# Turning half of the first pair's context among the last expert blocks, in memory lent from the blocks' side

## The chip, the core and the metric

The kernel runs on one core of a Trainium2 chip. The metric is the time of one execution in device microseconds, and times are compared as medians of several runs. One execution was also recorded by the hardware profiler; every position in microseconds below is counted from the start of that execution's span.

The engines are TensorE (PE; its weight loads are PEld), VectorE (DVE), ScalarE (ACT), GpSimd (POOL) and SyncE (SP), which issues most of the direct DMAs. Each engine works through its own list in order.

## What is computed

The program is a two-layer block on 32 sequences of 56 tokens (width 256), with a context of 1500 rows of 256 for each sequence. Cut to its four steps:

```python
x = x + L0_xattn(layernorm(x), ctx)          # a decayed scan over the context, averaged, as one row per sequence
x = x + L0_ffn(layernorm(x), ...)            # 16 experts, the 6 best of each token, hidden width 176
x = x + L1_xattn(layernorm(x), ctx, mask)    # softmax attention of 56 queries over 1500 context rows
x = x + L1_ffn(layernorm(x), ...)            # 2 experts, the best of each token, hidden width 1024
```

The third step is the one at which the change sits:

```python
scores = einsum('bsd,bmd->bsm', hidden_states, memory_tokens) * scale
scores = where(memory_mask[:, None, :], scores, -1e30)
attn = softmax(scores); readout = einsum('bsm,bmd->bsd', attn, memory_tokens)
```

## The kernel before

The 32 sequences are worked in 16 pairs, so that two times 64 query rows fill the 128 partitions. There are four stages: a first pass over all contexts (to about 200 us), the 99 expert blocks of the first expert layer (to about 456 us), the attention over the 16 pairs (to about 697 us), and the blocks of the second expert layer.

**The first expert layer.** `expert_blocks` walks over `NB0` = 99 blocks of 128 sorted rows. A step t multiplies block t by gate and up weights on PE (L723), ACT applies the silu (`sg`), DVE multiplies (`hs`, L735), PE turns `hs` of block t-1, DVE copies it out (`hT`, L743), and PE multiplies block t-2 by the down weights (`y`, L750). ACT copies `y` to `yb`, and SP writes `yb` to the array `ys0` in main memory (`ys<-yb`, L886). All weights lie in one tile, `w0_sb`, of 77,824 bytes in each partition. At the end of each step `side(t)` is called, which puts other work among the blocks in written order: the indices that bring the rows back (`ways`, working in the tiles `ra`, `rt1`, `t8s`), a row of constants (`zrow`) that is written to main memory, the gathers of the first five pairs' results by POOL (`results`, tiles `g` of the pool `res0`, summed by `added`), the queries of pairs 0 and 1, the first five contexts into the five slots of `ring`, and at step `NB0 - 4` the preparation of the second sort (`for_second_sort`).

**The attention.** A context of one sequence is a tile of 128 partitions by 3072 values (12 chunks of 256; 1.5 MB). There are eight slots: five in `ring` and three more, `extra0` to `extra2`, of the pool `at`, which takes memory that the blocks have used. `transposed(b, n)` is one DVE instruction (L1016) that turns half n of context b into a tile `cT`; `turn(p, n)` does so for the two contexts of a pair. `scores` multiplies 128 small matmuls for a pair (L1055): the first 64 read the `cT` tiles of half 0, the last 64 those of half 1. `mask_terms(p)` loads the pair's mask by SP (`mu`), and `mask_added` lets ACT make of it the tile `mf` of additive terms (L1038, L1043). `masked` adds `mf` on DVE and takes the maximum (L1068), `softmax` is ACT's exponential (L1080), `turned` turns the probabilities on PE (L1095), and `attend` multiplies them by the context (`op`, L1103) and then loads the pair four places on into the two slots that have come free. Of that loop the part around which the prediction turns is:

```python
cTs = [turn(0, 0), turn(0, 1)]
mask_added(mu_.pop(0))
for p in range(NP + 1):
    ...                                  # roots and query rows of pair p + 2, its mask
    sps = scores(cTs, xqs.pop(p))
    lo = turn(p + 1, 0)
    sc, mx = masked(sps)
    nb = softmax(sc, mx)
    cTs = [lo, turn(p + 1, 1)]
    ...                                  # attend pair p - 1, gathers of pair p + 5, queries of pair p + 2
    held = (p, turned(sc), nb)
    mask_added(mu_.pop(p + 1))
```

**What sets the order.** All engines are under a manual schedule: each engine's list is in the order in which the code is written, and only semaphores lie between engines. SP's list is one queue for masks, contexts and `ys<-yb`. Memory is taken by pools that are opened and closed like a stack. A pool that is opened over the memory of closed ones waits, with its first use by an engine, for all that still works in the closed ones under it. Before the attention `w0_sb` and the pools of the blocks are closed, and `so`, `pay`, `at`, `ctxT` (four `cT` tiles) and `res1` are opened over them, in this order. So `at` lies in what was `w0_sb`, and `ctxT` beyond it, over the blocks' working tiles, `yb` and `zrow` among them. At the start of the attention SP issues the two first masks and then the three `extra` contexts.

Of the kernel before, what the change touches and what calls it, by code (L numbers as in the profile page):

```python
# [8 lines left out]
F32 = mybir.dt.float32  # L9
U8 = mybir.dt.uint8  # L10
# [8 lines left out]
P = 128  # L19
B, S, D, T = 32, 56, 256, 1500  # L20
KD = D // P
NP = B // 2
TOK = 2 * S
NM, JM = 3, 4
NCH = NM * JM
TS = (T - P * JM) // (NM - 1)
TD = P * JM - TS
Q = 32
NE = D // Q
CW = NCH * D  # L30
NRING, NXTRA = 5, 3
E0, F0, K0 = 16, 176, 6
# [6 lines left out]
NE0 = 5  # L39
# [3 lines left out]
NB0 = (B * S * K0 + E0 * (P - 1)) // P  # L43
NY1 = 3
NB1 = B * S // P + 1
WP = 2 * D + 2
# [8 lines left out]
def xattn_ffn_kernel(  # L55
# [22 lines left out]
    nc = tc.nc  # L78
    V, A, PE, G = nc.vector, nc.scalar, nc.tensor, nc.gpsimd
# [3 lines left out]
    at2 = ctx.enter_context(tc.tile_pool(name="at2", bufs=2))  # L83
# [16 lines left out]
        out=before, in_=before, compare_op=ALU.is_gt, fill=0.0,  # L100
# [41 lines left out]
    slots = [ring[:, i, :].rearrange("p (j d) -> p j d", d=D) for i in range(NRING)]  # L142

    def load_ctx(b, c):
        nc.sync.dma_start(
            out=c.rearrange("p (m j) d -> p m (j d)", j=JM),
            in_=bass.AP(cx.tensor, b * T * D, [[JM * D, P], [TS * D, NM], [1, JM * D]]),
        )
# [56 lines left out]
    with tc.tile_pool(name="p1", bufs=1) as p1, tc.tile_pool(name="p3", bufs=3) as p3, tc.tile_pool(  # L205
        name="xn", bufs=4
    ) as xnp, tc.tile_pool(name="z", bufs=4) as zp, tc.tile_pool(name="p1_ps", bufs=5, space=PSUM) as ps, tc.tile_pool(
        name="p1_acc", bufs=2, space=PSUM
# [63 lines left out]
        q, r = divmod(TD, JM)  # L272
# [504 lines left out]
    def levels_of(p):  # L777

        return (TOK * (p + 1) - 1) // P + 1

    def results(pool, p, n, i):

        g = pool.tile([P, K0 // 2, D], F32, tag="g", name="g")
        for k in range(K0 // 2):
            G.indirect_dma_start(  # L785
                out=g[:, k, :], out_offset=None, in_=ys0[0 : n * P, :],
                in_offset=bass.IndirectOffsetOnAxis(
                    ap=back[:, p, 3 * i + k : 3 * i + k + 1], axis=0
                ),
            )  # L790
        return g
# [50 lines left out]
    def queries(pool, ps, tag, xn, half, xq=None):  # L842
# [10 lines left out]
        A.copy(xq[:, NE // 2 * half : NE // 2 * (half + 1), :].rearrange("p e c -> p (e c)"), tp)  # L853
        return xq

    mvq, xqs = {}, {}
    gd = at2.tile([P, D], F32, bufs=1, name="gd")
    toks = at2.tile([P, NP], F32, bufs=1, name="toks")
# [3 lines left out]
    with tc.manual_schedule(  # L862
        engines={ET.PE, ET.DVE, ET.Activation, ET.SP, ET.Pool}
    ), tc.tile_pool(name="f0", bufs=3) as wk, tc.tile_pool(name="f0r", bufs=1) as rt, tc.tile_pool(
        name="f0x", bufs=5
    ) as xbp, tc.tile_pool(name="res0", bufs=2) as resp, tc.tile_pool(
        name="f0_tr", bufs=2, space=PSUM
    ) as ptr, tc.tile_pool(name="f0_gu", bufs=2, space=PSUM) as pgu, tc.tile_pool(
        name="f0_ht", bufs=2, space=PSUM
    ) as pht, tc.tile_pool(name="f0_y", bufs=2, space=PSUM) as py:  # L870
        zrow = rt.tile([P, WP], F32, name="zrow")
        G.memset(zrow, 0.0)
        G.memset(zrow[:, WP - 1 : WP], float(FAR))

# [11 lines left out]
            nc.sync.dma_start(out=ys0[i * P : (i + 1) * P, :], in_=yb)  # L886


        ra = rt.tile([P, NP, E0], F32, name="ra")
        rt1 = rt.tile([P, NP, E0], F32, name="rt1")  # L890
        t8s = rt.tile([P, NP, 8], F32, name="t8s")

        def ways(a, b):
            n = b - a
# [25 lines left out]
        gs = {}  # L920
        ways_ = [f for a, b in ((0, NE0), (NE0, NP)) for f in ways(a, b)]

        mvs, steps = {}, {}

        gcol = rt.tile([P, KD], F32, name="gcol")

# [11 lines left out]

        def side(t):

            if t == NB0 - 4:
                for_second_sort()
            if t > 1:
                for _ in range(3):
                    if ways_:
                        next_ = ways_.pop(0)
                        next_()
            if t % 3 == 0 and 0 < t <= 3 * NRING:
                load_ctx(t // 3 - 1, slots[t // 3 - 1])
            if t % 3 == 0 and 0 < t - 3 * NRING <= NB1:  # L950
                j = t - 3 * NRING
                nc.sync.dma_start(
                    out=xs1.rearrange("(p j) d -> p j d", j=NB1)[:, j - 3 : j, :],
                    in_=zrow.unsqueeze(1).to_broadcast([P, 3, WP]),
                )
            for p in range(NE0):
                t0 = E0 * levels_of(p) + 4
                if t in (t0, t0 + 2):
                    gs.setdefault(p, []).append(
                        results(resp, p, E0 * levels_of(p), (t - t0) // 2)  # L960
                    )
                if t == t0 + 8:
                    added(p, gs.pop(p))
                if p >= 3:
                    continue
                if t == t0 + 14:
                    mvq[p] = stats1(xr[:, p, :])
                if p >= 2:
                    continue
                if t == t0 + 15:  # L970
                    steps[p] = list(roots_by_steps(mvq[p]))
                for _ in range(4):
                    if steps.get(p):
                        steps[p].pop(0)()
                if t == t0 + 20:
                    mvs[p] = query_rows(p, mvq[p])
                if t == t0 + 21:
                    xqs[p] = queries(at2, ptr, "tr", mvs[p], 0)
                if t == t0 + 22:
                    queries(at2, ptr, "tr", mvs[p], 1, xqs[p])  # L980
# [10 lines left out]
    payp = ctx.enter_context(tc.tile_pool(name="pay", bufs=7))  # L991
    with tc.manual_schedule(
        engines={ET.PE, ET.DVE, ET.Activation, ET.SP, ET.Pool}
    ), tc.tile_pool(name="at", bufs=1) as at, tc.tile_pool(
        name="ctxT", bufs=4
    ) as ctp, tc.tile_pool(name="res1", bufs=2) as resp, tc.tile_pool(
        name="at_sc", bufs=1, space=PSUM
    ) as psc, tc.tile_pool(name="at_pt", bufs=3, space=PSUM) as ppt, tc.tile_pool(
        name="at_o", bufs=1, space=PSUM
    ) as po:  # L1000
        for i in range(NXTRA):
            c = at.tile([P, NCH, D], F32, name=f"extra{i}")
            slots.append(c)
        NS = NRING + NXTRA
        mf = at.tile([P, NCH, P], F32, name="mf")
        G.memset(mf[:, JM:NCH, 0 : TD // JM + 1], -BIG)
        mus = [at.tile([P, T], U8, name=f"mu{i}") for i in range(2)]
        nbig = at.tile([P, 1], F32, name="nbig")
        G.memset(nbig, -BIG)
        gap = so.tile([1, 1], F32, name="gap")  # L1010
        A.preload_act_table_set("natural_log_exp_and_others")

        def transposed(b, n):

            cT = ctp.tile([P, NCH, NE // 2, Q], F32, tag="cT", name="cT")
            V.transpose(  # L1016
                out=cT.rearrange("p j e q -> p j (e q)"),
                in_=slots[b % NS][:, :, P * n : P * n + P],
            )
            return cT  # L1020

        def mask_terms(p):

            mu = mus[p % 2]
            nc.sync.dma_start(
                out=mu, in_=bass.AP(mask.tensor, 2 * p * T, [[T, 2], [0, 64], [1, T]])
            )
            return mu

        mu_ = {p: mask_terms(p) for p in range(2)}  # L1030
        for b in range(NRING, NS):
            load_ctx(b, slots[b])

        def mask_added(mu):
            q, r = divmod(TD, JM)
# [196 lines left out]
                tc.add_to_no_dep_group("xs1", g.ins)  # L1232

        def turn(p, n):
            return [transposed(2 * p + h, n) for h in range(2)]

        def apart():

# [4 lines left out]
                results(*queue[sent[0]])  # L1243
                sent[0] += 1

        cTs = [turn(0, 0), turn(0, 1)]
        mask_added(mu_.pop(0))
        mvs, four, late = {}, [], []
        held = None
        for p in range(NP + 1):  # L1250
            if p == NP - 1:
                order_of_blocks()

            if p + 2 < NP:
                roots(mvq[p + 2])
            if p - 2 in mvs:
                roots(mvs[p - 2])
            if p + 2 < NP:
                xn = query_rows(p + 2, mvq.pop(p + 2))
                mu_[p + 2] = mask_terms(p + 2)  # L1260
            if p - 2 in mvs:
                sort_norm(p - 2, mvs.pop(p - 2))
            if p < NP:
                sps = scores(cTs, xqs.pop(p))
                if p + 1 < NP:
# [3 lines that stand above are left out]
                if p + 1 < NP:  # L1269
                    cTs = [lo, turn(p + 1, 1)]  # L1270
                inverse(mx, nb)
            if held:
                op = attend(held[0], held[1])
                mvs[held[0]] = sort_rows(held[0], op, held[2])
                held = None

            for i in range(2):
                if p + NE0 < NP:
                    fresh = results(resp, p + NE0, NB0, i)
                if late:  # L1280
                    half_added(*late.pop())
                if p + NE0 < NP:
                    late.append((p + NE0, fresh))
            if p + 3 < NP:
                mvq[p + 3] = stats1(xr[:, p + 3, :])
            if p + 2 < NP:
                xqs[p + 2] = queries(at2, ppt, "pt", xn, 0)
                queries(at2, ppt, "pt", xn, 1, xqs[p + 2])
            if four:
                sort_place(*four[0], sort_rank(four.pop()[1], ppt, "pt"))  # L1290
            if 0 <= p - 2 < NP:
                sort_gate(p - 2)
                if (p - 2) % GP == GP - 1:
                    o = p - 2 - GP + 1
                    four.append((o, sort_four(o)))
            if p < NP:
                held = (p, turned(sc), nb)
            if p + 1 < NP:
                mask_added(mu_.pop(p + 1))
            if p == NP - 1:  # L1300
                for i in range(NY1):
                    apart()
                    rows_of1(i, payp, "pay")
# [110 lines left out]
```

## Time and profile before

| | |
|---|---|
| median of six runs | 885.63 us (882.16 to 890.86) |
| profiled execution | 879.96 us, its span 878.2 us |
| mean granted TensorE clock | 0.959 |
| PE busy | 801.5 us, 91% of the span |
| DVE, ACT, POOL busy | 55%, 39%, 45% |
| last matmul of the first blocks, first scores | 455.6 us, 460.15 us |
| direct loads on SP's queue | 139.55 MB, 45.6% of 16 DMA engines' span |

How to read it: the share of busy time is a mean over stages that have different limits. The change sits at one seam, between two stages in which PE is nearly always busy, so the lines to look at are those around 456 us, engine by engine. The chain of waits names, from the end backwards, what released each step. In the timeline the square brackets hold the idle time before an instruction and what ended it. The granted clock is the share of full speed at which TensorE was let run.

### The profile page before, as it was taken

To read this page: it belongs to the slowest core of one execution; us is meant where nothing else is said; L and a number is where in the kernel's file an instruction comes from. 1 tells how busy PE (TensorE), PEld (TensorE's weight loads), DVE (VectorE), ACT (ScalarE), POOL (GpSimd) and SP (SyncE) were. 2 spreads that over 40 slices of the span, in tenths; PEclk is the share of its full clock that TensorE was granted. 3 is DMA by queue.
4 is the path that set the end of the run, shared out by engine and by line. 5 is a ranking of instruction groups with operands and counts; after the bars stand their busy time and mean duration, and the time that the engine had idled before them with its cause. 6 is when DMAs were issued, how large, how long until landed. Compare 5 with 4: busy or idle time off the path is not lost.

```text
span 878.2 us, 18685 instructions
## 1 busy us (share of the span) xinstructions
PE 801.5 (91%) x6658; PEld 527.9 (60%) x6658; DVE 481.1 (55%) x1419; ACT 343.3 (39%) x902; POOL 398.7 (45%) x497
## 2 busy tenths in 40 slices
PE   4688888878999999999978999899998999999997
PEld 4345555545777777777754666555655556665664
DVE  3487777873542424332237888778979333323332
ACT  0133333323444444444435675764766311111110
POOL 4455565425347656565717886288400230111110
PEclk9799999968999999999997999899999999999999
DMA  9999999933987534344528796797975720110010
GB/s 264 348 397 382 334 391 354 322 124 105 318 293 248 153 108 138 103 142 116 124 73 297 244 329 229 244 324 262 318 249 179 255 85 13 36 37 27 29 37 12
DMA packets 77820, 176.58 MB, mean 201 GB/s; under 512 B 7795, under 2 KB 41476, under 8 KB 77732
## 3 DMA queue, kind: packets, MB, share of 16 engines
q1 hardware_dynamic: 64756, 139.55, 45.6%
q0 software_dynamic: 12976, 35.85, 14.2%
q8 instruction: 56, 0.92, 0.4%
q14 instruction: 32, 0.26, 0.1%
HBM read 150.83 MB, written 25.20 MB: 200 GB/s over the span
## 4 chain that ended last, share of the span: by engine, by line
PE 56%; DMA 10%; issue 4%; DVE 4%; ACT 2%; POOL 0%; POOLq 0%; SPq 0%; DVEq 0%; ACTq 0%
PE gu L723 23%; PE y L750 15%; DMA extra<-in_cx 6%; PE sp L1055 5%; PE tp L741 4%; PE op L1103 4%; PE tp L166 3%; DMA ring<-in_cx 2%; PE tp L1095 2%; DVE cT L1016 1%; DVE sc L1068 1%; PE tp L849 1%; ACT sc L1080 1%; DMA xb<-xs,idx 1%; DMA xb<-xn,idx 0%
## 5 line engine op out<-in xcount | busy, mean ns | idle before, releaser
L729 ACT ACTIVATE sg<-gu 128x176 f32<-128x176 f32 (+1 forms) x159 | 54.3, 342 | 214.7 <-PE gu L723 214.6
L877 POOL DMA_INDIRECT xb<-xn,idx x99 | 93.8, 947 | 92.9 <-PE tp L166 71.7
L723 PE MATMUL gu<-w_sb,xT 128*128 x396 | 133.8, 459 | 2.3 <-DMA xb<-xn,idx 1.2
L735 DVE SCALAR_TENSOR_TENSOR hs<-sg,wgt,gu 128x176 f32<-128x176 f32 x99 | 39.4, 398 | 158.5 <-ACT sg L729 158.5
L723 PE MATMUL gu<-ring,xT 128*128 x240 | 112.9, 593 | 1.2 <-ACT mv L814 1.2
L785 POOL DMA_INDIRECT g<-ys,back x96 | 91.2, 950 | 34.5 <-issue 24.8
L750 PE MATMUL y<-w_sb,hT 88*128 x396 | 101.8, 379 | 0.0
L1055 PE MATMUL sp<-cT,xq 32*64 32x384 f32 x2048 | 93.3, 508 | 4.6 <-DVE cT L1016 4.6
L723 PEld LDWEIGHTS gu<-w_sb,xT 128*128 128x128 f32 x396 | 74.0, 189 | 29.5 <-ACT xT L168 2.8
L733 DVE TENSOR_TENSOR hs<-sg,gu 128x256 f32<-128x256 f32 x60 | 25.2, 421 | 115.6 <-ACT sg L729 115.6
L1016 DVE STREAM_TRANSPOSE cT<-ring 128x1536 f32<-128x1536 f32 x40 | 69.4, 1761 | 24.7 <-PE sp L1055 14.8
L741 PEld LDWEIGHTS tp<-ident,hs 128*88 128x88 f32 (+1 forms) x318 | 40.9, 129 | 60.6 <-issue 47.6
L1349 POOL DMA_INDIRECT out<-ob,ti x15 | 14.8, 989 | 129.5 <-DVE ob L1346 129.2
L1055 PEld LDWEIGHTS sp<-cT,xq 32*64 32x64 f32 x2048 | 44.8, 139 | 45.7 <-issue 20.1
L750 PEld LDWEIGHTS y<-w_sb,hT 88*128 88x128 f32 x396 | 67.3, 190 | 5.6 <-issue 0.2
L168 ACT COPY xT<-tp 128x256 f32<-128x256 f32 x130 | 48.4, 372 | 48.1 <-PE tp L166 47.2
L743 DVE COPY hT<-tp 88x256 f32<-88x256 f32 (+1 forms) x159 | 65.9, 415 | 0.6 <-PE tp L741 0.6
L723 PEld LDWEIGHTS gu<-ring,xT 128*128 128x128 f32 x240 | 45.4, 190 | 33.5 <-issue 29.2
L1103 PE MATMUL op<-ring,pT 128*64 128x256 f32 x480 | 64.8, 381 | 0.0
L741 PE MATMUL tp<-ident,hs 128*88 128x128 f32 (+1 forms) x318 | 60.8, 273 | 1.3 <-DVE hs L733 1.3
L750 PE MATMUL y<-ring,hT 128*128 x240 | 61.7, 380 | 0.0
L1180 POOL DMA_INDIRECT xs<-pay,to x16 | 15.8, 987 | 88.3 <-DVE cum L1177 57.0
(267 smaller groups left out, 1362.3 us busy)
## 6 DMA issues: line engine op xcount, KB each, us to landing
ring<-in_cx SPq DMA_DIRECT2D x52, 1536.0 KB
extra<-in_cx SPq DMA_DIRECT2D x12, 1536.0 KB
ys<-yb SPq DMA_DIRECT2D x99, 128.0 KB
xs<-zrow SPq DMA_DIRECT2D x5, 771.0 KB
mu<-in_mask SPq DMA_DIRECT2D x16, 187.5 KB
w_sb<-in_wg SPq DMA_DIRECT2D x2, 1408.0 KB
w_sb<-in_wu SPq DMA_DIRECT2D x2, 1408.0 KB
xn<-xn SPq DMA_DIRECT2D x16, 128.0 KB
```

Of the source, the lines that this page charges most:

```text
L168: A.copy(xT.rearrange("p k c -> p (k c)"), tp[:, 0 : KD * P])
L723: PE.matmul(gu[:, 0 : 2 * fp], lhsT=xT[i][:, k, :], rhs=w[:, bass.ds(at[i] + (u * piece + k * 2 * fp), 2 * fp)], start=(k == 0), stop=(k = ...
L729: A.activation(sg, gu[:, 0:fp], AF.Silu)
L735: V.scalar_tensor_tensor(hs[i, u], sg, wgt[:, i : i + 1], up, ALU.mult, ALU.mult)
L741: PE.transpose(tp[0:h, c * P : (c + 1) * P], a[:, c * h : (c + 1) * h], ident)
L743: V.tensor_copy(hT[i, u], tp[0:h, 0 : 2 * P])
L750: PE.matmul(y[i][:, 0:D], lhsT=a[:, c * P : (c + 1) * P], rhs=w[0:h, bass.ds(at[i] + (u * piece + doff + c * D), D)], start=(u == 0 and c ...
L785: G.indirect_dma_start(out=g[:, k, :], out_offset=None, in_=ys0[0 : n * P, :], in_offset=bass.IndirectOffsetOnAxis(ap=back[:, p, 3 * i + k ...
L877: G.indirect_dma_start(out=xb, out_offset=None, in_=xn0, in_offset=bass.IndirectOffsetOnAxis(ap=idx[:, i : i + 1], axis=0),)
L1016: V.transpose(out=cT.rearrange("p j e q -> p j (e q)"), in_=slots[b % NS][:, :, P * n : P * n + P],)
L1055: PE.matmul(sps[a][64 * h : 64 * h + 64, 0 : Q * NCH], lhsT=xq[Q * a : Q * a + Q, e, 64 * h : 64 * h + 64], rhs=cTs[e // 4][h][Q * a : Q * ...
L1103: PE.matmul(op[64 * h : 64 * h + 64, 0:D], lhsT=pT[:, j, 64 * h : 64 * h + 64], rhs=slots[(2 * p + h) % NS][:, j, :], start=(j == 0), stop ...
```

## The change

One tile of 12,288 bytes in each partition, `lent`, is opened in the blocks' pool `f0r`. `zrow`, `ra`, `rt1`, `t8s` and two fixed gather buffers (in place of the pool `res0`) are cut out of it. When these have done their work, the same memory takes `cT0`, the two tiles of half 0 of pair 0. The two transposes are written into `side`, at steps `NB0 - 5` and `NB0 - 4`. `for_second_sort` goes from step `NB0 - 4` to `NB0 - 10`. The first mask is loaded at step `NB0 - 8`, into a tile that now lies beside the constants. In the attention only half 1 of pair 0 is turned ahead of the loop; the three `extra` contexts are issued ahead of the second mask; and the pools are opened in another order, `ctxT` and `res1` ahead of `at`, with `mf` first in `at`. With that `ctxT`, `res1`, `mf` and `extra0` and `extra1` lie in what was `w0_sb`, `extra2` over its end and the blocks' working tiles, and `at`'s last tiles (`sc`, `pT`) over `lent`. No instruction is added or left out.

```diff
-    def results(pool, p, n, i):
-        g = pool.tile([P, K0 // 2, D], F32, tag="g", name="g")
+    def results(g, p, n, i):
...
+    def transposed(b, n, cT):
+        V.transpose(
+            out=cT.rearrange("p j e q -> p j (e q)"),
+            in_=slots[b][:, :, P * n : P * n + P],
+        )
+        return cT
+    mus = [at2.tile([P, T], U8, bufs=1, name="mu0")]
...
+        lent = rt.tile([P, CW], F32, name="lent")
+        cT0 = lent.rearrange("p (h j e q) -> p h j e q", h=2, j=NCH, q=Q)
+        gb = [lend(K0 // 2 * D).rearrange("p (k d) -> p k d", d=D) for _ in range(2)]
+        zrow = lend(WP)
...
-            if t == NB0 - 4:
+            if t == NB0 - 10:
                 for_second_sort()
...
+            if t == NB0 - 8:
+                mu_[0] = mask_terms(0)
+            if NB0 - 5 <= t < NB0 - 3:
+                h = t - NB0 + 5
+                transposed(h, 0, cT0[:, h])
...
-    ), tc.tile_pool(name="at", bufs=1) as at, tc.tile_pool(
-        name="ctxT", bufs=4
-    ) as ctp, tc.tile_pool(name="res1", bufs=2) as resp, tc.tile_pool(
+    ), tc.tile_pool(name="ctxT", bufs=4) as ctp, tc.tile_pool(
+        name="res1", bufs=2
+    ) as resp, tc.tile_pool(name="at", bufs=1) as at, tc.tile_pool(
...
+        mus.append(at.tile([P, T], U8, name="mu1"))
-        mu_ = {p: mask_terms(p) for p in range(2)}
         for b in range(NRING, NS):
             load_ctx(b, slots[b])
+        mu_[1] = mask_terms(1)
...
-        cTs = [turn(0, 0), turn(0, 1)]
+        cTs = [[cT0[:, h] for h in range(2)], turn(0, 1)]
```

## The prediction, made before the changed kernel was run

> **What bounds the kernel now.** I read the page first, then the chain of waits, then the timeline of each engine at the seam between the first expert blocks and the attention, and last the windows table there. PE is busy 91% of the span and holds 56% of the chain. The change touches one place where it waits: the seam. Chain, columns start, length, work:
>
> ```profile
> 453.67 1.94 PE y L750 x8
> 456.07 1.68 DMA ys<-yb
> 458.27 3.45 DVE cT L1016 x2
> 461.76 4.18 PE sp L1055 x48
> ...
> 473.43 2.82 PE tp L1095 x12
> 476.25 6.85 PE sp L1055 x128
> 483.10 5.33 PE op L1103 x48
> 489.46 1.39 PE tp L1095 x12
> ...
> 532.44 20.84 DMA extra<-in_cx
> ```
>
> The last block's matmuls end at 455.6; the first scores start at 460.15 and really run from 461.76, because DVE waits for the last `ys<-yb` to land and then turns two tiles. From 532 on the chain shows context loads too. Timeline of DVE and ACT (start, length, work, idle before and its releaser), then of SP's queue:
>
> ```profile
> 442.02 0.41 DVE L743 COPY hT<-tp 88x256 f32<-88x256 f32 x1
> 444.20 0.40 DVE L735 SCALAR_TENSOR_TENSOR hs<-sg,wgt,gu 128x176 f32<-128x176 f32 x1 [1.76 <-ACT sg L729]
> 458.27 6.76 DVE L1016 STREAM_TRANSPOSE cT<-ring 128x1536 f32<-128x1536 f32 x4 [4.14 <-DMA mu<-in_mask]
> 465.97 3.44 DVE L1016 STREAM_TRANSPOSE cT<-ring 128x1536 f32<-128x1536 f32 x2 [0.94 <-PE sp L1055]
> 465.24 1.92 ACT L1038 ACTIVATE mf<-mu,nbig 128x512 f32<-128x512 uint8 x3 [7.89 <-DMA mu<-in_mask]
> 476.77 1.91 ACT L1038 ACTIVATE mf<-mu,nbig 128x512 f32<-128x512 uint8 x3
> ```
>
> ```profile
> 456.49 1.24 SPq L1025 DMA_DIRECT2D mu<-in_mask  x2
> 457.77 8.28 SPq L145 DMA_DIRECT2D extra<-in_cx  x3
> 488.46 0.90 SPq L145 DMA_DIRECT2D ring<-in_cx  x2
> ```
>
> Four transposes of 1.7 us stand between blocks and scores, two masks are issued ahead of three contexts, and DVE has a hole of 1.76 us in every block. Windows (PE, PEld, DVE, ACT, POOL busy, granted clock, DMA share, GB/s):
>
> ```profile
> 457.00:458.00 1.00, 0.00 (x0) 0.00 (x0) 0.00 (x0) 0.35 (x1) 0.00 (x0) 1.00 0.34 104
> 459.00:460.00 1.00, 0.00 (x0) 0.00 (x0) 1.00 (x2) 0.00 (x0) 0.82 (x1) 0.50 0.11 40
> 463.00:478.00 15.00, 11.71 (x156) 6.62 (x148) 11.95 (x21) 9.53 (x18) 10.53 (x13) 0.73 1.01 369
> ```
>
> While PE idles the clock falls to 0.50, and the first scores pay for it; at 463 to 478 the DMA engines are full with the three contexts.
>
> **Removed at the seam.** (1) The two transposes of pair 0's first half leave the gap. `lent`'s readers are the scores themselves, and their matmuls wait only for blocks' work, so they can start at 455.7. One pair's scores take 5.35 us at full clock (chain, at 490.85), a half 2.7: 458.4. (2) The pool `ctxT` moves down into what `w0_sb` held, so the second half's transposes no longer wait for `ys<-yb` (458.27) but for the last y matmul: 455.75 plus 3.45 is 459.2. (3) The second half of the scores then ends at 459.25 plus 2.65, 461.9, instead of 469.05. (4) With two of pair 0's four tiles elsewhere, pair 1's first two transposes find free buffers at once; they stand ahead of the masking on DVE: 459.2 plus 3.45 is 462.65. So masking starts at 462.65 instead of 469.33 (465.97 plus 3.44): **6.7 us earlier**. The first mask, loaded eight steps before the blocks' end, is no bound: its ACT work needs `nbig`, whose memset now waits for the first half of the scores (458.4); about 458.9 plus 2.2 is 461.1.
>
> The clock: PE's gap shrinks from 4.6 us to about 0.1, so I count the scores at full clock. In one-microsecond windows it fell 3.2 us after PE stopped here (455.6, 458.8), and once 1.6 us after (556.2, 557.8). [...] I keep the slow clock there as before (2.82 and 6.85 us): scores of pair 1 end at 476.4, `op` of pair 0 at 481.75.
>
> **Added: the wait of the contexts and of the second mask.** Pool `at` now lies over `lent`, so its first uses, the three `extra` loads among them, wait for the first half of the scores (458.4) and for the last `ys<-yb` (458.27): 458.4 instead of 457.77. Behind the first `extra` in SP's queue wait the other two, `mu1`, the next masks and the ring loads. No masks go ahead of them now. The ring pair issued at 488.46 reached full rate in about 2.5 us, these three in 5.0 (462.75). The 2.5 us between them say that this queue works in order and the masks held the contexts up. I take 2.5: full rate at 460.9, 1.8 earlier than before, drained at 476.7 instead of 478.5. `mu1` follows: 188 KB at 369 GB/s is 0.5, and I allow 1.3 with its landing: 478.0. The bounds are 0.5 (477.2) and the 8.75 us that the first mask took from issue to use in this trace (485.5). ACT wants it at 476.77 less 6.7, so ACT waits about 8 us, and behind it on ACT stand the roots and query rows of pair 3 and pair 1's exponential. Mask work ends at 480.1 (2.1 long); masking to exp was 2.38 (483.95 to 486.33), exp 1.67: pair 1's transposes start at 484.3. They began at 489.46, when PE was free; **5.2 us earlier**, so the wait gives back 1.5 of the 6.7.
>
> [...] No row here shows a mask behind contexts.
>
> **Moved into the blocks, at nothing.** Two transposes at steps NB0-5 and NB0-4. Each starts after hT (442.43) and takes 1.73 to 1.78; the hole until the next hs is 1.76. The cover is that hole; without it hs comes 0 to 1.8 us late, of which PE's turn of that hs, 1.5 us after it, absorbs most: 0 to 0.3 each, 3.5 us in all if nothing covered them. Their waits are over: POOL's last add into `lent` ended at 437.27 in this trace. `for_second_sort` costs PE 1.09 us (step 443.65 to 447.23 against 2.49) at NB0-4, and the same six steps earlier. The first mask's load is one of SP's DMAs among `ys<-yb`, in a stretch at 73 GB/s. POOL's gathers for the attention start at 459 instead of 458.87; its work on pair 5's rows ended at 476.9, needed after 500. All zero; nothing is taken out of the blocks, so no gain, and 3.5 as the loss.
>
> **The rest of the loop.** Ring loads are issued at the end of `op`: 481.8 instead of 488.46, while pairs come 5.2 us earlier, so loads keep their lead or gain 1.5. DVE waits 12.8 us for contexts in all (7.1 and 5.7, seven waits). I take zero; bounds: all 5.2 lost again to such waits, or some 3 of them gone.
>
> **Sum.** 6.7 less 1.5 less 0 less 0 is 5.2; I forecast 5.1 us. The profiled execution is 879.96 (span 878.2, 1.8 around it), so about 874.9; it lies 5.7 below the median of the six runs, and I take the difference off the median: 885.63 less 5.1 is 880.5.
>
> **Rivals.** *A, the second mask is late* (slower). Each microsecond of `mu1` after 478.0 costs one. At 485.5 the mask ends at 487.6, the gain is 5.2 less 7.5, and PE, idle from 482 on, falls to half clock: tp and scores cost 1.4 and 1.5 more. That is 5.2 lost: 890.8. Against no change it decides from about 480.3 with the clock, 483.2 without. For it: the first mask took that long with no context in front of it. Against it: contexts shared the engines then. *B, the head start is eaten by the loop* (no change): the loads, not PE, set pairs 6 to 13, and the wait before 553 grows by what PE gained. Left are 0 to 3: about 884. For it: 20.84 us of load in the chain at 532; against: each load is issued by an `op` that is also earlier. *C, more*: the seam keeps 6.7 as `mu1` lands by 476.5, and 3 us of load waits go: 876.0. *D, the transposes among the blocks do not hide*: 3.5 less gain, 884.
>
> **How the numbers follow.** About 0.5% (4.4 us) is what a measurement of this kernel can tell from no change. My case 0.40 and C 0.10 are faster; B 0.25 and D 0.05 are no change, and so is half-way A, 0.05; A in full 0.15. Range: C's 876.0 below; above, A part of the way, 889.0. What is left out is A in full and what lies beyond C, together some 2 in 10. The likeliest case alone spans 878 to 881.
>
> **What would show it.** Right: PE's gap at the seam near 0.1 us and no slow clock at the first scores; first masking 6 to 7 us after the last y; `mf<-mu` of pair 1 waiting for `mu<-in_mask` some 8 us; pair 1's transposes some 29 us after the last y, 33.9 before; hs in the two steps unmoved. Wrong: that wait over 12 us, or context waits well over 12.8, or the block steps longer than 2.6.

## The result, and the profile after

The changed kernel took 882.81 us (median of 34 runs, 878.33 to 893.97), the kernel before, run beside it, 885.34 (71 runs, 879.23 to 896.62). The ratio is 0.9979, its 95% interval 0.9964 to 0.9994: a gain of 1.9 us, 0.5 to 3.2 (the two medians lie 2.5 apart). The forecast of 5.1 had the sign; of the size a good third came. The profiled execution took 882.6 us with a span of 880.9. It is longer than the one of before (878.2), but 2.5 us of that come before anything of the change: the last y of the blocks ends at 458.14 instead of 455.60, as the first blocks' rows arrived later at 204 to 209 us: PE waited 1.08 and 1.34 us for `xb` there, in place of once 1.23, and the granted clock was 0.55 and 0.60 in the windows from 206 and 208, where it had been 1.00 (the kernel before with masks in halves, further below, has it at 458.10). So below every position at the seam is counted from the end of the last y, with a plus sign.

The chain of waits of the changed kernel at the seam (start, length, work):

```profile
456.21 1.94 PE y L750 x8
458.21 0.38 ACT yb L911
458.61 2.36 DMA ys<-yb
...
462.74 19.59 DMA mu<-in_mask
482.36 1.91 ACT mf L1051 x3
...
486.90 1.68 ACT sc L1093 x2
488.62 2.82 PE tp L1108 x12
491.45 6.06 PE sp L1068 x128
497.51 5.33 PE op L1116 x48
...
530.61 20.82 DMA extra<-in_cx
```

In the place of two DVE transposes and the first scores the chain now holds one load of 188 KB for 19.59 us. Behind it pair 1's probability transposes and pair 2's scores run slowly (2.82 and 6.06, where the next pair takes 1.38 and 5.35). The wait for `extra<-in_cx` from 530.61 has the length that it had before. The timeline, DVE and ACT first, then SP's queue and PE (start, length, work, idle before and its releaser):

```profile
445.34 0.40 DVE L735 SCALAR_TENSOR_TENSOR hs<-sg,wgt,gu 128x176 f32<-128x176 f32 x1 [1.76 <-ACT sg L729]
445.99 1.76 DVE L865 STREAM_TRANSPOSE lent<-ring 128x1536 f32<-128x1536 f32 x1
447.83 0.40 DVE L735 SCALAR_TENSOR_TENSOR hs<-sg,wgt,gu 128x176 f32<-128x176 f32 x1
450.32 0.40 DVE L735 SCALAR_TENSOR_TENSOR hs<-sg,wgt,gu 128x176 f32<-128x176 f32 x1
458.17 6.76 DVE L865 STREAM_TRANSPOSE cT<-ring 128x1536 f32<-128x1536 f32 x4 [1.50 <-DMA ys<-yb]
482.36 1.91 ACT L1051 ACTIVATE mf<-mu,nbig 128x512 f32<-128x512 uint8 x3 [9.95 <-DMA mu<-in_mask]
```

```profile
461.24 1.45 SPq L145 DMA_DIRECT2D extra<-in_cx  x3
462.74 22.26 SPq L858 DMA_DIRECT2D mu<-in_mask  x3
485.09 1.04 SPq L145 DMA_DIRECT2D ring<-in_cx  x2
```

```profile
458.06 2.84 PE L1068 MATMUL sp<-lent,xq 32*64 32x384 f32 x64
460.69 3.78 PE L1068 MATMUL sp<-cT,xq 32*64 32x384 f32 x64
486.53 1.97 PE L848 MATMUL tp<-ident,xn 128*128 128x128 f32 x8 [3.75 <-ACT xn L829]
```

The transposes among the blocks fill DVE's hole exactly: hs still comes every 2.49 us (445.34, 447.83, 450.32). The first scores start as the last y ends. The mask makes ACT wait 9.95 us, and behind ACT PE idles 3.75 us. In the windows (PE, PEld, DVE, ACT, POOL busy, granted clock, DMA share of 16 engines, GB/s) the clock is 1.00 at the first scores, low ahead of pair 0's probability transposes (469), as it was before the change (0.50 from 473 to 478 there), and low once more where the mask comes late (487):

```profile
458.00:459.00 1.00, 1.00 (x25) 0.59 (x32) 0.83 (x1) 0.77 (x2) 0.00 (x0) 1.00 0.40 137
469.00:470.00 1.00, 1.00 (x5) 1.00 (x6) 1.00 (x1) 0.86 (x2) 0.29 (x1) 0.51 1.02 365
477.00:478.00 1.00, 1.00 (x22) 0.48 (x8) 1.00 (x1) 0.00 (x0) 0.91 (x2) 1.00 0.78 257
479.00:480.00 1.00, 1.00 (x12) 0.66 (x10) 0.00 (x0) 0.00 (x0) 0.77 (x1) 1.00 0.28 99
487.00:488.00 1.00, 1.00 (x7) 1.00 (x6) 1.00 (x1) 1.00 (x1) 0.69 (x2) 0.50 0.82 223
```

The contexts' full rate ended at about +19.7 (477.8), and the mask was used at +24.2. The trace's list of DMA packets tells the two apart, as a context's packets have 4096 bytes and a mask's 1500, one for each of its 128 rows: the mask's rows were started from +18.5 to +23.6, and the last packet of the three contexts at +23.1. Followed along the seam, the kernels compare so:

| after the last y, us | before | after | gained |
|---|---|---|---|
| first masking on DVE | +13.73 | +6.71 | 7.0 |
| pair 1's probability transposes | +33.70 | +30.48 | 3.2 |
| second `op` starts | +40.52 | +39.30 | 1.2 |
| last `op` ends | +241.00 | +240.58 | 0.4 |

The lines behind the last two rows of the table, before and then after:

```profile
496.12 5.40 PE L1103 MATMUL op<-ring,pT 128*64 128x256 f32 x48
691.20 5.40 PE L1103 MATMUL op<-extra,pT 128*64 128x256 f32 x48
```

```profile
497.44 5.40 PE L1116 MATMUL op<-ring,pT 128*64 128x256 f32 x48
693.32 5.40 PE L1116 MATMUL op<-extra,pT 128*64 128x256 f32 x48
```

A gain of 7.0 us shrinks in three steps. The last of them lies in the loop: by the eleventh `op` the two kernels are level (+172.5 before, +173.0 after). What DVE waited for before `cT` in the changed kernel (us in all, times), after 5.7 and 7.1 before:

```profile
  DMA ring<-in_cx: 9.3, 6
  DMA extra<-in_cx: 8.0, 5
```

### The profile page after: what moved, and what is told of

Same layout as the page of the kernel before. It is cut to its first block, busy times and chain, and to the rows that moved or that the text cites. A ratio compares the mean times of both kernels' runs of the same rounds, so it can differ in the third digit from the quotient of the medians.

```text
span 880.9 us, 18688 instructions
## 1 busy us (share of the span) xinstructions
PE 801.4 (91%) x6658; PEld 528.2 (60%) x6658; DVE 481.5 (55%) x1419; ACT 344.3 (39%) x902; POOL 398.8 (45%) x497
## 4 chain that ended last, share of the span: by engine, by line
PE 65%; DMA 13%; DVE 8%; issue 5%; ACT 3%; POOL 3%; SPq 0%; POOLq 0%; DVEq 0%; ACTq 0%
PE gu L723 24%; PE y L750 14%; DMA extra<-in_cx 7%; PE acc L294 5%; PE sp L1068 4%; PE tp L741 4%; PE tp L166 4%; PE op L1116 3%; DMA ring<-in_cx 2%; DMA mu<-in_mask 2%; PE tp L1108 2%; DVE sc L1081 1%; POOL xn L459 1%; PE bp L435 1%; DVE oh L539 1%
## 5 line engine op out<-in xcount | busy, mean ns | idle before, releaser
L1068 PE MATMUL sp<-cT,xq 32*64 32x384 f32 x1984 | 86.9, 493 | 0.1
L865 DVE STREAM_TRANSPOSE cT<-ring 128x1536 f32<-128x1536 f32 x38 | 66.0, 1762 | 21.1 <-PE sp L1068 10.3
L784 POOL DMA_INDIRECT g<-ys,back x66 | 62.8, 952 | 19.7 <-issue 13.3
L1068 PEld LDWEIGHTS sp<-cT,xq 32*64 32x64 f32 x1984 | 42.3, 135 | 37.6 <-issue 13.8
L1193 POOL DMA_INDIRECT xs<-pay,to x16 | 15.8, 987 | 88.5 <-DVE cum L1190 58.1
```

The costliest lines, as they stand in the source:

```text
L784: G.indirect_dma_start(out=g[:, k, :], out_offset=None, in_=ys0[0 : n * P, :], in_offset=bass.IndirectOffsetOnAxis(ap=back[:, p, 3 * i + k ...
L865: V.transpose(out=cT.rearrange("p j e q -> p j (e q)"), in_=slots[b][:, :, P * n : P * n + P],)
L1068: PE.matmul(sps[a][64 * h : 64 * h + 64, 0 : Q * NCH], lhsT=xq[Q * a : Q * a + Q, e, 64 * h : 64 * h + 64], rhs=cTs[e // 4][h][Q * a : Q * ...
```

## The experiments

**Theory and rival.** The theory was the prediction's own, with its second mask corrected: the mask behind the contexts takes the gain away at the seam, and once it is out of their way the gain arrives. The rival: the loop is at the limit of its loads and eats every head start.

### Where the second mask is loaded

*The mask ahead of the contexts:*

```diff
+        mu_[1] = mask_terms(1)
         for b in range(NRING, NS):
             load_ctx(b, slots[b])
-        mu_[1] = mask_terms(1)
```

> The changed kernel with one edit: the second mask is issued ahead of the three extra contexts, not behind them. In the changed kernel ACT waited 9.95 us for that mask, and PE then stood still for 3.75 us and fell to half clock. Theory 1 (the mask was late because it stood behind the contexts, and that ate the head start): the wait goes, masking of pair 1 starts 20 to 22 us after the last y instead of 26.3, the probabilities of pair 1 are turned 26.5 to 28 us after it instead of 30.5, scores of pair 2 run at full clock, and the time is 2.5 to 5 us below the changed kernel's 882.8, about 879. Rival (the loop's context loads set its time, so the seam does not count): the same at the seam, but the time stays within 1 us of 882.8. Also possible: the mask holds up the contexts by some 2.5 us as it did in the kernel before; then pair 2's transposes wait for extra0 for up to 2 us.

Measured: 885.06 us beside 885.67 for the kernel before, ratio 1.0007 (0.9974 to 1.0041). No wait for the mask was left, the second `op` started at +32.36, 8.2 us ahead of before, and nothing of it arrived: the last `op` ended at +241.86. DVE's waits for contexts had grown to

```profile
  DMA extra<-in_cx: 13.3, 6
  DMA ring<-in_cx: 10.5, 7
```

The rival held, with a median 2.3 us above the 882.8 that it had named. *The mask among the blocks*, in memory that the first sort has done with:

```diff
+    spl = const.tile([P, 3, NP, E0], F32, name="spl")
+    sel, pos, lvl = (spl[:, i] for i in range(3))
...
+    mus.append(spl.rearrange("p a q e -> p (a q e)")[:, 0 : T // 4].bitcast(U8))
...
+            if t == NB0 - 7:
+                mu_[1] = mask_terms(1)
```

> The changed kernel with one edit: the second mask is loaded at step NB0-7, right after the first, into constants that are dead by then, so at the seam SP issues only contexts. Theory 1: no wait for a mask at all and contexts as early as in the changed kernel (full rate about 2.8 us after their issue); probabilities of pair 1 turned 26 to 27.5 us after the last y, time 3 to 5.5 us below 882.8, about 878.5, and not above that of the version with the mask ahead. Rival (the loop eats it): within 1 us of 882.8.

Measured: 878.54 us, ratio 0.9910 (0.9880 to 0.9940). The seam is that of the kernel above (second `op` at +32.32), yet here 5.9 of its 8.2 us are left at the last `op` (+235.08). Two kernels with one seam lie 6.5 us apart. What differs is the queue: there a mask stands in front of the contexts, here none (its tile lies elsewhere too; with halves, below, the same two places end 1.3 us apart). The last packet of the three contexts was started at +24.8 there and at +22.4 here. The eleventh `op` starts at +172.9 with the mask ahead, level with the kernel before and the changed one, and here at +163.8. So the rival was right in part: the loop is at its limit, and one mask's load ahead of the contexts is enough to matter to it; but with that mask out of the queue, most of a head start comes through the same loop of whole masks.

### Each mask as two loads

The mask's source pattern begins with a dimension of two, one step for each sequence of the pair. The load is slow: masks alone moved at 48 GB/s in the kernel before, on a share of 0.13 of the 16 engines (the window stands below), where the contexts moved at 369. Whether two loads whose patterns begin with 64 rows move faster was tried:

```diff
-        nc.sync.dma_start(
-            out=mu, in_=bass.AP(mask.tensor, 2 * p * T, [[T, 2], [0, 64], [1, T]])
-        )
+        for h in range(2):
+            nc.sync.dma_start(
+                out=mu[64 * h : 64 * h + 64],
+                in_=bass.AP(mask.tensor, (2 * p + h) * T, [[0, 64], [1, T]]),
+            )
```

*In the changed kernel:*

> The changed kernel with one edit: every mask is loaded by two DMAs, one for each sequence of the pair, of 64 rows each, instead of one whose outermost dimension is 2. Theory 2 (a mask moves slowly of itself: 188 KB took 4.5 us from the end of the contexts to its use, 42 GB/s, about what two of 16 DMA engines carry at 369 GB/s in all; so each mask keeps two engines 4 us longer, and a context is not there before its last engine is): the second mask is used 1 to 2.5 us after the contexts instead of 4.5, and context waits of DVE in the loop, 17.3 us in the changed kernel's profile, fall below 6; time 8 to 14 us below 882.8, about 872. Rival (the mask only stands in the queue behind the contexts, its shape costs nothing): the seam as it was, within 1.5 us of 882.8, or a little slower for 16 more issues on SP of 0.4 us each.

Measured: 868.61 us, ratio 0.9828 (0.9783 to 0.9874). DVE waited for no context any more. But the second mask at the seam was as late as before, used at +24.37 after a wait of 10.44 us: that part of the expectation fell. The rows of the masks of pairs 1 and 2 were started between +18.0 and +24.3, the contexts' last packet at +22.5. So the masks went beside the contexts' tail; what held them there was not shown, as the packets do not name engines. *In the kernel before:*

> The kernel before with the same one edit, each mask in two DMAs of 64 rows. Theory 2: the first mask is there sooner (8.75 us from issue to use before, now 3 to 5, though at the seam the scores bound the masking and nothing is gained there), and DVE's context waits in the loop, 12.8 us before, fall below 5; time 7 to 12 us below 885.3. Rival: within 1.5 us of 885.3.

Measured: 866.77 us, ratio 0.9796 (0.9753 to 0.9839), more than had been reckoned. The first mask was used 3.65 us after its issue instead of 8.75, and the waits for contexts were gone. So with halves the change loses what it had gained: the kernel before is now no slower than the changed one. The windows show the rates. Whole masks alone on the DMA engines, in the kernel before:

```profile
459.00:459.50 0.50, 0.00 (x0) 0.00 (x0) 0.50 (x1) 0.00 (x0) 0.50 (x1) 0.50 0.13 48
```

Halves alone, in the kernel before with halves (its repeat):

```profile
462.00:462.50 0.50, 0.00 (x0) 0.00 (x0) 0.50 (x1) 0.00 (x0) 0.08 (x1) 0.50 0.43 153
```

A share of 0.13 of 16 engines is two engines' worth, and at 48 GB/s 188 KB take about 4 us. Halves reach 153 GB/s on 0.43, three times as much. The share is a mean over half a microsecond and does not say over how many engines a load was spread; nor was it parted whether the pattern or the number of loads made the difference.

### Whether the gain arrives when the loop has room

The next kernels join halves with an early second mask. In one of them the two transposes also come later, to part the place among the blocks from the rest of the change:

```diff
-            if NB0 - 5 <= t < NB0 - 3:
-                h = t - NB0 + 5
+            if NB0 <= t < NB0 + 2:
+                h = t - NB0
```

and in one the three extra contexts get a pool of their own, opened ahead of the others:

```diff
+    ), tc.tile_pool(name="ex", bufs=1) as exp_, tc.tile_pool(
...
-            c = at.tile([P, NCH, D], F32, name=f"extra{i}")
+            c = exp_.tile([P, NCH, D], F32, name=f"extra{i}")
```

They were first run in a stretch in which the kernel before itself took 936.12 us.

Mask among the blocks and halves: 

> The changed kernel with both aids together: the second mask among the blocks, and each mask as two loads of 64 rows. Theory: the two act in different places, so the seam is that of the kernel with the mask among the blocks (pair 1's probability transposes about 25.5 us after the last y, against 32.2 in the kernel before with halves), the loop has no wait for contexts, and all of those 6.7 us arrive: 866.8 less 6.7 is about 860. Rival: the loop eats the head start whatever its cause, as it did when the mask was put ahead of the contexts: 865 to 867.

Transposes later: 

> The same kernel with the two transposes of the first half put behind the blocks' last DVE work (steps 99 and 100) instead of steps 94 and 95; all that is otherwise freed stays. Theory: DVE's last hT copy ends near 2 us before the last y, so the first half is turned by +1.6, the second by +5.0, pair 1's first two by +8.5, and the first masking starts at +8.5 instead of +6.7: 1.8 us lost, about 862. Rival: the place among the blocks is worth all 3.5 us of the two instructions (863.5), or nothing, as the mask's or another wait comes last (860).

Mask ahead of the contexts, with halves: 

> The changed kernel with the second mask put ahead of the three contexts, and each mask as two loads of 64 rows. Theory: with whole masks this won 8 us at the seam and lost them in the loop, because the loop's loads were at their limit; with halves the limit is gone, so the win stays: about 860, as the kernel with the mask among the blocks. Rival: the contexts held up behind the mask cost it in any case: 865 or more, with waits of DVE for contexts in the loop.

Contexts in a pool of their own: 

> Mask among the blocks, halves, and the three extra contexts in a pool of their own that lies in the weights' memory, so that their loads need not wait for the first half of the first scores and are issued about 3 us earlier. Theory: no wait for contexts is left, so earlier contexts bring nothing: 860, within 1 of the kernel without that pool. Rival: the contexts of pairs 2 and 3 still end a wait somewhere: 1 to 3 us less.

Measured, in this order: 939.40, 942.31, 940.67 and 939.51 us, ratios 1.0036 (1.0003 to 1.0068), 1.0057 (1.0025 to 1.0090), 1.0023 (0.9993 to 1.0053), 1.0047 (1.0011 to 1.0084). None of the expectations holds there. Something else bounds the kernel: PE stands still for times that the profile puts down to `issue`, its name for a wait that ends in nothing it shows. PE's timeline of the first one at the seam:

```profile
509.11 2.79 PE L1110 MATMUL tp<-ident,sc 128*128 128x128 f32 x12 [8.24 <-issue]
511.83 8.40 PE L1070 MATMUL sp<-cT,xq 32*64 32x384 f32 x127
```

There is a wait of 8.24 us, and then scores of which 127 of 128 take 8.40 us (all take 5.42 elsewhere, and 6.92 at the slow clock of the kernel before). The cause is open. The chip alone does not explain it: these runs and their repeat bear the same chip number (10), against what the next expectation says, and in the repeat the kernel before took 885.99 us. The runs tell of that stretch only. The pool of the contexts' own was not run again, and stays open. The other three were run once more, with the kernel before with halves among them:

> The changed kernel with the second mask among the blocks and each mask as two loads of 64 rows, on another chip. [...] Theory: where the kernel before takes about 885 us, pair 1's probability transposes start about 25.5 us after the last y, no wait for contexts is left, and the time is about 860, 6 to 7 below the kernel before with halves. Rival: the loop eats the head start: 865 to 867, the same as the kernel before with halves.

> The kernel before with each mask as two loads of 64 rows, beside the other kernels of this batch on one chip. Expected as measured first: ratio 0.980 to the kernel before, about 867 where that takes 885. If the gain of the halves hung on the chip, the ratio comes out nearer to 1.

> As the kernel with the mask among the blocks and halves, but the two transposes of the first half behind the blocks' last DVE work. Its first run put the transposes at 1.55 us before the last y's end, the second half at +1.80, the first masking 1.7 later than the kernel with the transposes among the blocks. Theory: 1.7 us lost, about 862. Rivals: 3.5 lost, or none.

> The changed kernel with the second mask ahead of the three contexts, and halves. Theory: the 8 us that this order wins at the seam stay, since the loop's loads are no longer at their limit: about 860. Rival: contexts held up behind the mask cost it again: 865 or more, with DVE waiting for contexts in the loop.

| | us (6 runs) | ratio to before (885.99) | first masking | second `op` | last `op` ends |
|---|---|---|---|---|---|
| before, halves | 866.82 | 0.9778 (0.9738 to 0.9817) | +13.27 | +38.97 | +225.98 |
| mask in blocks, halves | 861.79 | 0.9762 (0.9708 to 0.9816) | +6.71 | +32.34 | +220.18 |
| the same, transposes late | 863.93 | 0.9763 (0.9714 to 0.9812) | +8.44 | +35.25 | +221.74 |
| mask ahead, halves | 863.54 | 0.9748 (0.9702 to 0.9794) | +6.71 | +32.36 | +221.50 |

None of the four had a wait for contexts in the loop. The ratios are too wide to part them. The traces, one of each, do: of 6.6 us at the second `op`, 5.8 reach the last `op`; the medians differ by 5.0. Of the 18 runs of the three changed kernels 14 lie at 861.3 to 865.0 and four at 869.3 to 872.2; of the 12 runs of before with halves (six here, six earlier) eleven lie at 865.7 to 868.3 and one at 875.0. So the gain arrives in most runs, and its size is known to a few microseconds only. PE's timeline of before with halves and of the mask among the blocks with halves, at the same place:

```profile
490.82 1.55 PE L1097 MATMUL tp<-ident,sc 128*128 128x128 f32 x12
492.30 5.42 PE L1057 MATMUL sp<-cT,xq 32*64 32x384 f32 x128
```

```profile
483.21 1.55 PE L1110 MATMUL tp<-ident,sc 128*128 128x128 f32 x12
484.69 5.42 PE L1070 MATMUL sp<-cT,xq 32*64 32x384 f32 x128
```

The same matmuls, 1.55 and 5.42 us long in both, from +32.15 and from +25.51. With the mask ahead of the contexts, which had lost all 8.2 us while masks were whole, the gain now stays. The transposes' place among the blocks is worth 1.7 us at the first masking, as expected, and about as much at the end (1.6 at the last `op`, 2.1 in the medians). The larger part, 4.8 us of 6.6 at the first masking, comes with what the two versions share: the freed memory, the order of the pools and the early masks, which were not parted further. The version with the mask among the blocks and halves has the lowest median, some 24 us below the kernel before and, across batches, 21 below the changed one.

### What held the mask, and what the clock cost

Three kernels more, each the changed one with whole masks. *Without POOL's gathers of pairs 5 to 8*, *with the mask behind the first of the three contexts*, and *with PE kept busy in its gap*:

```diff
-                    results(fresh, p + NE0, NB0, i)
+                    if p < 4:
+                        G.memset(fresh, 0.0)
+                    else:
+                        results(fresh, p + NE0, NB0, i)
```

```diff
         for b in range(NRING, NS):
             load_ctx(b, slots[b])
-        mu_[1] = mask_terms(1)
+            if b == NRING:
+                mu_[1] = mask_terms(1)
```

```diff
+            if p == 1:
+                d = ppt.tile([P, 512], F32, tag="pt", name="d")
+                for _ in range(30):
+                    PE.matmul(d[:, 0:D], lhsT=ident, rhs=gd, start=True, stop=True)
```

> The changed kernel without POOL's gathers of the expert rows of pairs 5 to 8 (left out: their tiles are set to zero instead), so that nothing but contexts and the mask moves after the seam. Theory: the contexts' tail, from 477.5 to 482.4 in the changed kernel at a third to a half of the engines, is that of the engines that also served the gathers; without them the contexts drain in one piece, 4.7 MB at some 400 GB/s from +7.5 on, and the mask is used at about +20 instead of +24.2. Rival: the tail is the mask's own transfer (188 KB as 128 rows), and the use stays at +23 to +24.

> The changed kernel with the second mask issued behind the first of the three contexts instead of the third. Theory: the queue's order sets its landing; two contexts fewer ahead of it are 3.1 MB, 7.5 to 8.5 us at 370 to 420 GB/s, so it is used at about +16 instead of +24.2, with a wait of 1 to 2 us left. Rival: its own transfer beside full DMA engines takes the time: +20 or later.

> The changed kernel with 30 matmuls of 128x256 added on TensorE behind the first op, about 3.3 us at 0.11 us each, whose result nobody reads; they fill most of the gap of 3.75 us ahead of pair 1's probability transposes. Theory: the clock does not fall, those transposes take 1.4 instead of 2.82 and the next scores 5.4 instead of 6.06, so the second op starts 2 us earlier than +39.3; in the time of the whole kernel between nothing and 2 us, since loads are the loop's limit. Rival: the clock falls all the same, or the second op starts no earlier because another wait is last: no change.

These too first fell in such a stretch (before: 938.86 us; they took 928.38, 957.90 and 953.96, the first two in a single run, the last with a ratio of 1.0213, 1.0137 to 1.0289). The mask was used at +21.4 without gathers and at +24.4 with all of them; behind one context it had landed before ACT came to it at +20.5. The 30 matmuls were mis-sized: they took 13.22 us instead of 3.3 (0.44 each; the 0.11 was that of `op`, whose matmuls the profile lists as 128\*64 and not 128\*128, and did not carry over), and overfilled the gap. So all three were run again, with 8 matmuls:

> The changed kernel without POOL's gathers of the expert rows of pairs 5 to 8 (left out, their tiles set to zero). Its first look had the mask used at +21.4 after a wait of 7.14, against +24.4 with the gathers in the same batch. Theory: the gathers' share of the engines makes the tail, +20 to +21.5 again. Rival: +24 as in the changed kernel.

Measured: 870.91 us (one run), mask used at +21.60 after 8.00 us. The windows now show contexts and mask apart:

```profile
474.00:475.00 1.00, 1.00 (x32) 0.51 (x24) 0.00 (x0) 0.00 (x0) 0.84 (x3) 0.95 1.01 418
475.00:476.00 1.00, 1.00 (x40) 0.49 (x32) 0.10 (x1) 0.00 (x0) 0.94 (x2) 1.00 0.71 286
...
479.00:480.00 1.00, 1.00 (x12) 0.66 (x10) 0.33 (x1) 0.00 (x0) 1.00 (x2) 1.00 0.14 51
480.00:481.00 1.00, 1.00 (x14) 0.64 (x12) 0.00 (x0) 0.32 (x1) 0.92 (x2) 1.00 0.13 50
```

The contexts' full rate ends at about +16.6 instead of +19.7, and their last packet is started at +18.0 instead of +23.1: the gathers held them up by 3 to 5 us. After that the mask goes on alone at 50 GB/s on a share of 0.13 to 0.14, two engines' worth, and is used 5 us after the full rate has ended, just past the range expected. Both theory and rival are right in part: the contexts' tail is lengthened by the gathers, and the mask's own transfer takes the rest.

> The changed kernel with the second mask issued behind the first of the three contexts. Its first look only bounded the landing (there by +20.45, when ACT came to it). Theory: landing by the queue's order, used at +14 to +16.5. Rival: its own transfer beside full DMA engines holds it to +18 or later.

Measured: 884.41 us (one run), used at +18.69 after 4.45 us. That is the rival's range: 5.5 us earlier for two contexts fewer ahead of it, not 8. The mask's 128 rows were started from +8.3 to +18.0, 9.7 us beside the contexts, so the order of the queue counts, and its own transfer more. Waits for contexts rose to 25.8 us (15.8 and 10.0), as with the mask ahead of all three (23.8).

> The changed kernel with 8 matmuls of 128x256 added on TensorE behind the first op, about 3.5 us at the 0.44 us that each of 30 took, whose result nobody reads. Theory: TensorE then idles under 1 us ahead of pair 1's probability transposes, the clock does not fall, those transposes take 1.5 instead of 2.82 and the next scores 5.4 instead of 6.06, so the second op starts at about +37.2 instead of +39.3; in the time of the whole kernel 0 to 2 us, since loads are the loop's limit. Rival: the clock falls all the same, or another wait is last: +39.3.

Measured: 884.44 us, ratio 0.9977 (0.9950 to 1.0003). PE's timeline:

```profile
483.43 3.72 PE L1304 MATMUL d<-gd,ident 128*128 128x256 f32 x16
487.12 1.09 PE L848 MATMUL tp<-ident,xn 128*128 128x128 f32 x8
489.21 1.62 PE L1108 MATMUL tp<-ident,sc 128*128 128x128 f32 x12 [1.00 <-ACT sc L1093]
490.76 5.42 PE L1068 MATMUL sp<-cT,xq 32*64 32x384 f32 x128
```

The transposes take 1.62 instead of 2.82 and the scores 5.42 instead of 6.13, and the second `op` starts at +37.27 instead of +39.30, though the mask was as late (+24.11). So the clock's fall costs 2.0 us at the seam. None of them arrive: the eleventh `op` starts at +172.7, level with the others, the last ends at +241.30, and the ratio is that of the changed kernel.

## Why the prediction was right or wrong

**Right: the seam's transposes and the first scores.** Forecast was a first masking at +7.05 in place of +13.73; it came at +6.71. (469.33, behind the +13.73, is the masking's own row; the sum set beside it, 465.97 plus 3.44, is 469.41. The steps to pair 1's transposes add up to 484.15, not 484.3. Neither slip matters.) PE's gap of 4.55 us closed (the first scores start at 458.06, the last y ends at 458.14), and the scores of pair 0 ran at full clock (1.00 in the windows from 458 to 462), their first half from `lent` in 2.84 us. The slow clock that the prediction kept is the one ahead of pair 0's probability transposes, 2.82 us for these and 6.85 for the scores of pair 1; it stayed (0.51 from 469; 2.79 and 5.73 us).

**Right: the work moved into the blocks costs nothing.** hs did not move. A block's period of 2.49 us has just the room: a hole of 1.76 us, a transpose of 1.76.

**Wrong, the term that was mis-sized: the landing of the second mask.** The drain was reckoned at 476.7, 21.1 after the last y; it came at +19.7. From there the prediction allowed 1.3 us, with 188 KB at 369 GB/s, the rate of all engines. It was 4.5, so the mask came 1.8 later than forecast (+24.2, not +22.4). The term's fault was its rate: the mask's rows took 5.1 us, from +18.5 to +23.6, in place of 0.5. Alone, as without the gathers, a mask moves at 50 GB/s, which is 3.8 us by itself; here contexts and gathers moved beside it. Nor did it wait for all of the contexts, as the order of the queue had been read: its rows began 4.6 us before their last packet. The first mask's row of 8.75 us, kept as an upper bound and set down to shared engines, pointed the right way: its rows took 5.5 us, from +2.3 to +7.8, for the most part before the contexts were at full rate (from +7.15). The slow rate could have been read from the windows of before (48 GB/s at 459, and 40 in the prediction's own fence). A faster rate alone would not have been enough here: halves were as late (+24.37), beside contexts whose last packet was started at +22.5. Halves without gathers were not tried.

**Wrong, a cost left out: the clock in the wait.** The prediction priced it for rival A alone. PE idled 3.75 us, the clock fell to 0.50, and that costs 2.0 us, as the kernel with 8 matmuls shows. The two terms, 1.8 and 2.0, leave 1.4 of the 5.2 us by the sum; 1.2 were measured at the second `op`.

**Wrong in its reason: the loop at zero.** It took 0.8 of that 1.2 again, in single profiles (two of before with halves differ by 0.6 at the last `op`), and DVE's waits for contexts went from 12.8 to 17.3 us. The sum of these waits is no measure of the loss: with PE kept busy it was 12.5. More telling is what happened to a larger head start: 8.2 us were lost in full with the mask ahead, 2.0 with PE kept busy, and in both, as in the changed kernel and the one before, the eleventh `op` starts at +172.5 to +173.0. With the second mask out of the queue, 5.9 of 8.2 came through; whether 5.2 would have, had the mask landed as forecast, no run shows. So rival B, put at 0.25, names most of the mechanism, and rival A, in part, adds to it. What slowed the loads was in neither. The halves show that it was the masks; how, was not shown. An estimate of the author's: if a mask lies on two of the 16 engines, as its share of 0.13 suggests, these carry a sixteenth each of two contexts (3.15 MB at some 400 GB/s, the rate of full windows: 7.9 us) and then the mask (3.9 at 48 GB/s), 11.8 in all, with the gathers on top, in a pair that PE does in 13.1. With masks in halves the waits vanish, and the change is worth about 5 us once its own second mask is out of the way. That this is close to the forecast is luck: the changed kernel did not have these conditions.

## What to carry to other kernels

Before a transfer is priced at the rate of the window around it, look for a place in the trace where one of its kind moves alone: here a mask did 48 GB/s, not the 369 of the contexts, and with each mask as two loads at 153 GB/s DVE's waits for the contexts, 17.3 us, were gone. A head start at the door of a loop can be lost inside it (with the mask ahead of the contexts all 8.2 us were), so look first for the waits inside the loop, and remove those: here they were worth some 19 us, the head start 2 beside them and about 5 without them. And when a wait replaces another, price the clock in it: here 2.0 us behind a gap of 3.75.

## What had not been expected

- One load of a 188 KB mask as 2 x 64 rows ran at 48 to 51 GB/s on 0.13 to 0.14 of the engines; as two loads of 64 rows at 153 GB/s on 0.43. Over the whole kernel that was worth 18.9 us (866.77 beside 885.67), more than anything else tried.
- The granted clock fell in a PE gap of 3.75 us, and not where 1.0 us was left of it. Ahead of pair 0's transposes it fell though no gap there was longer than 2.17 us (0.51 in the window from 469); gaps of 1.27 and 2.17 us with 1.09 us of transposes between them were enough here.
- POOL's gathers held three contexts of 1.5 MB up by 3 us at the seam (full rate until +19.7, not +16.6; last packet at +23.1, not +18.0), and without the gathers of four pairs the kernel took 870.91 us in one run, 12 less than the changed kernel.
- For whole stretches one and the same program can be some 50 us slower: the kernel before took 936 and 939 us in two of them, and a changed version, profiled there, has an idle time of PE of 8.24 us put down to `issue` alone. What brings such a stretch on, no run shows.
